# Layer 3 of a four-layer network on one core: query blocks of 10 rows in place of 8, with two reorderings of the masking

## The chip, the cores and the metric

The kernel runs on one core of a Trainium2 chip. A core has five engines that run at the same time, each with its own instruction stream: PE (TensorE, matmuls), DVE (VectorE, elementwise work), ACT (ScalarE, copies and activations), POOL (GpSimd, [...]) and SP (SyncE), which here issues nearly all DMAs. [...] The metric is the device time of one execution in microseconds. Of the kernel before there are three timed runs: 3771.21, 3783.98 and 3786.39 us; the median is 3783.98.

## The reference, cut to what matters

The input is `x` of 4 images, 256 channels, 48 x 48 pixels. Four layers each compute `x = x + layer(groupnorm(x))`. Layers 0 to 2 are convolutions (one with a per-pixel softmax over 49 taps, one with binarized and one with ternarized weights) and are not touched here. Layer 3 is a linear attention over box windows, with 8 heads of 32 channels:

```python
q = jax.nn.sigmoid(Wq x); k = jax.nn.sigmoid(Wk x); v = (Wv x) / max(norm(v), 1e-12)
Ik, Ikv = integral(k), integral(outer(k, v))            # summed-area tables
for w in (1, 2, 4):
    ws = 48 // w                                        # box of 48, 24 or 12 pixels a side
    wk, wkv = box(Ik, ws), box(Ikv, ws)                 # sums over the box around each pixel
    attn = einsum('bdhw,bdfhw->bfhw', q, wkv)
    norm = einsum('bdhw,bdhw->bhw', q, wk)
    outs.append(attn / (norm + 1e-6))
return x + (Wout concat(outs) + bout)
```

So for each query pixel and each of three window sizes, the output is the sum over all key pixels in the box of (q . k) v, divided by the sum over the box of q . k.

## The kernel before, in words

**How layer 3 computes it.** Instead of the large table of outer products, the kernel forms the scores q . k for blocks of queries against tiles of keys, multiplies them with 0/1 masks that say which keys lie in the box of which query (one mask for each window size), and multiplies the masked scores with v. The normalizers come from box sums of k alone, in a separate job.

**Tiles and blocks.** A key tile (a, c) is 8 rows by 16 columns, 128 keys on the 128 partitions; there are 6 row groups a and 3 column groups c. A query block is `RB` = 8 rows by 48 columns, 384 queries; there are 6. For each image b (4), each half of the channels ct (2, four heads each) and each query block rb, the class `Block` goes through the key tiles that any of its queries sees in the widest window. `rows_seen` and `cols_seen` give the rows and columns of the block that see something of the tile with window `wi`; `HALVES` = 24, 12, 6 are the half sizes. A tile is *near* when the smallest window sees it (`many`), otherwise *far*. `tiles_of` orders them, near and far alternating while both last, columns in the order 1, 0, 2. With 8-row blocks there are 12, 15, 18, 18, 15 and 12 tiles in the six blocks, 90 for one (b, ct), 720 in all.

**One tile.** `scores` makes, for each of two pairs of heads, a PSUM tile `s` of two banks by one matmul per head (contraction over 32 channels, four heads side by side in the array). The pool of `s` has two buffers, so each pair has one. fp32 matmuls appear in the profile as two instructions each. `masked` then makes SBUF tiles `sm0`, `sm1`, `sm2`, one per window size, for each pair:

- `copy`: where every query row and column sees the whole key tile in the widest window (`full`; columns f0 to f1), no mask is needed and ACT copies `s` to `sm0`.
- `widest`: DVE masks the remaining column strips from `s` to `sm0`. If the tile is not `full`, DVE masks all of it and ACT copies nothing.
- `middle`: for near tiles, DVE masks `s` to `sm1`.
- POOL masks the smallest window from `sm0` to `sm2` in near tiles, and the middle one from `sm0` to `sm1` in far tiles that see it.

Before the change these are issued in this order (first and second are the pairs of heads):

```python
copy(*first)
middle(*second)
copy(*second)
middle(*first)
widest(*first)
widest(*second)
```

`sums` multiplies v (32 columns per head, four heads side by side) with the masked scores and adds into three PSUM banks `acc`, one per window. It runs `LAG` = 2 tiles behind `scores`: in the main loop at the end of the file, step n issues the scores and masks of tile n, then the sums of tile n-2. [...] four by `s`, three by `acc`, one (`st`) by everything else.

**The rest of layer 3, interleaved.** Every step also calls `advance`, which moves a list of generator jobs on by one step each; a job says with `yield` how many steps it wants to pause (`FETCH` is 4). The engines then run their streams in the order of issue. The jobs are:

- `Projection` for the next image (q, k, v from x3), on PE, ACT, DVE and POOL, written to DRAM.
- `k_sums`: box sums of k (DVE scans, POOL adds), written to `kb_d`.
- `norms`, one for each 8 rows: loads the box sums above (`nhi`) and below (`nlo`), subtracts and multiplies with q on POOL for each channel half, sums over the channels of a head on PE, takes the reciprocal on DVE and writes it to `r_d`.
- `prepare` and `finish` for each block with ct = 1: load the block's other half (`o`), the residual (`res`) and the reciprocals (`rc`), multiply on DVE, then the output projection `out_ps` on PE (12 matmul calls in two pieces), add the bias and residual on DVE, and store.

`until` and `wait_for` hold the program's order of issue, not an engine: a step whose data is not yet issued advances the jobs until it is. Key tiles are loaded by `load_kv` (`ks`, `vs`) into a pool of 12 buffers each, the next half's at the points in `LOADS`; query rows by `load_q`.

Layer 3's first `s` matmul starts at 1429.5 us of the profiled execution and its last at 3751.0, so it is some 62% of the time. All helper calls carry line 142 in the profile, so groups are told apart by tile names.

Of the kernel before, what the change touches and what calls it, by code (L numbers as in the profile page):

```python
# [80 lines left out]
NKT = NRB * NKC  # L81

# [63 lines left out]
def conv_preact_kernel(  # L146
# [76 lines left out]
    o_d = [dram.tile([NRB, P, NW * NB], F32, tag=f"o{b}", name=f"o_d{b}") for b in range(B)]  # L223
    n_d = [dram.tile([NRB, HEADS, NW, NB], F32, tag=f"n{b}", name=f"n_d{b}") for b in range(B)]
    r_d = [dram.tile([NRB, HEADS, NW, NB], F32, tag=f"r{b}", name=f"r_d{b}") for b in range(B)]
# [1257 lines left out]
    with (  # L1483
        tc.tile_pool(name="wts3", bufs=1, reuse_waits="tile") as wts,
        tc.tile_pool(name="kvp", bufs=2 * NRB, reuse_waits="tile") as kvp,
# [21 lines left out]
        zeros = wts.tile([P, NB], BF16, name="zeros")  # L1507
# [63 lines left out]
        def norms(b, rb):  # L1571


            sums = []

            def load(ct):
                chans = slice(ct * P, (ct + 1) * P)
                hi = scr.tile([P, NW, RB, W], F32, tag="nhi", name="nhi")
                lo = scr.tile([P, NW, RB, W], F32, tag="nlo", name="nlo")
                qf = scr.tile([P, RB, W], F32, tag="nq", name="nq")  # L1580
                sync.dma_start(
                    out=qf.rearrange("p r w -> p (r w)"),
                    in_=q_d[b][chans, rb * NB : (rb + 1) * NB],
                )
                for wi, h in enumerate(HALVES):

                    y0 = rb * RB + h - 1
                    n = max(0, min(RB, H - y0))
                    if n > 0:
                        sync.dma_start(  # L1590
                            out=hi[:, wi, 0:n], in_=kb_d[b][wi, chans, y0 : y0 + n, :]
                        )
                    if n < RB:
                        sync.dma_start(
                            out=hi[:, wi, n:RB],
                            in_=kb_d[b][wi, chans, H - 1 : H, :].to_broadcast([P, RB - n, W]),
                        )

                    y0 = rb * RB - h - 1
                    n = min(RB, max(0, -y0))  # L1600
                    if n < RB:
                        sync.dma_start(
                            out=lo[:, wi, n:RB], in_=kb_d[b][wi, chans, y0 + n : y0 + RB, :]
                        )
                return hi, lo, qf

            last = min(rb + HALVES[0] // RB, NRB - 1)
            yield from wait_for(
                *((what, b, ct, at) for what, at in (("kb", last), ("q", rb)) for ct in range(NCT))
            )  # L1610
            loaded = [load(ct) for ct in range(NCT)]
            yield FETCH
            for hi, lo, qf in loaded:
                for wi, h in enumerate(HALVES):
                    n = min(RB, max(0, h + 1 - rb * RB))
                    if n < RB:
                        pool.tensor_sub(hi[:, wi, n:RB], hi[:, wi, n:RB], lo[:, wi, n:RB])
                yield 1
                for wi in range(NW):
                    pool.tensor_mul(hi[:, wi], hi[:, wi], qf)  # L1620
                sums.append(hi)
                yield 1
            yield 1
            yield from bank(1)
            ps = ps_m.tile([P, 512], F32, tag="st", name="norm_ps")
            for ct in range(NCT):
                for wi in range(NW):
                    pe.matmul(
                        ps[D * wi : D * (wi + 1), 0:NB],
                        head_sel[:, ct, :],  # L1630
                        sums[ct][:, wi].rearrange("p r w -> p (r w)"),
                        start=(ct == 0),
                        stop=(ct == NCT - 1),
                    )
            yield 1
            ns = scr.tile([D * NW, NB], F32, tag="ns", name="ns", bufs=1)
            act.copy(ns, ps[0 : D * NW, 0:NB])
            yield 1
            for wi in range(NW):
                sync.dma_start(out=n_d[b][rb, :, wi, :], in_=ns[D * wi : D * wi + HEADS])  # L1640
            nn = HEADS * NW * NB // P
            nr = scr.tile([P, nn], F32, tag="nr", name="nr")
            flat = [d[b][rb].rearrange("h w n -> (h w n)") for d in (n_d, r_d)]
            sync.dma_start(out=nr, in_=flat[0].rearrange("(p n) -> p n", n=nn))
            yield FETCH
            dve.tensor_scalar_add(nr, nr, ATTN_EPS)
            dve.reciprocal(nr, nr)
            yield 1
            sync.dma_start(out=flat[1].rearrange("(p n) -> p n", n=nn), in_=nr)
            made.add(("norm", b, rb))  # L1650
# [12 lines left out]
        def load_q(b, ct, rb):  # L1663
            qs = qp.tile([P, RB, W], F32, tag="qs", name="qs")
            sync.dma_start(
                out=qs.rearrange("p r w -> p (r w)"),
                in_=q_d[b][ct * P : (ct + 1) * P, rb * NB : (rb + 1) * NB],
            )
            return qs

        def rows_seen(wi, a, rb):

            h = HALVES[wi]
            return (
                max(0, a * RB - h + 1 - rb * RB),
                min(RB, a * RB + RB + h - rb * RB),
            )
# [5 lines left out]
        class Block:  # L1683


            def __init__(self, b, ct, rb, qs):
                self.b, self.ct, self.rb, self.qs = b, ct, rb, qs
                self.tiles = tiles_of(rb)
                self.todo = [
                    [(a, c) for a, c in self.tiles if seen(wi, a, rb)] for wi in range(NW)  # L1690
                ]
                self.accs = self.stage = None

# [18 lines left out]
            def masked(self, a, c, ss):  # L1712
# [8 lines left out]
                            [P, 2, RB, min(W, KC + 2 * HALVES[wi])],  # L1721
# [15 lines left out]
                def times_mask(engine, wi, rows, cols, dst, src):  # L1737
                    mr = rb * RB + rows[0] - (a * RB - HALVES[wi] + 1)
# [14 lines left out]
                full = abs(a - rb) * RB + RB <= HALVES[0]  # L1753
# [7 lines left out]
                def copy(s, tiles):  # L1761
                    if full:
                        act.copy(
                            view(tiles, 0, (r0, r1), (f0, f1)), s[:, :, :, f0 - c0 : f1 - c0]
                        )

                def widest(s, tiles):
# [3 lines left out]
                    for p0, p1 in ((c0, f0), (f1, c1)):  # L1771
                        if p0 < p1:
                            of_banks(s, tiles, 0, (r0, r1), (p0, p1))

# [4 lines left out]
                middle(*second)  # L1779
                copy(*second)  # L1780
                middle(*first)
                widest(*first)
# [13 lines left out]
            def begin(self):  # L1796
                self.accs = [
                    ps_acc.tile([P, NB], F32, tag=f"acc{i}", name=f"acc{i}") for i in range(NW)
                ]
                self.stage = op.tile([P, NW, NB], F32, tag="stage", name="stage")  # L1800

                for acc in self.accs[1:]:
                    pe.matmul(acc, zeros[:, 0:P], zeros, start=True, stop=False)
# [23 lines left out]
        def tiles_of(rb):  # L1827
# [4 lines left out]
                for a in sorted(range(NRB), key=lambda a: abs(a - rb))  # L1832
# [8 lines left out]
        def prepare(i):  # L1841

            b, ct, rb = order[i]
            yield from wait_for(("norm", b, rb))
            yield from take("o")
            o = op.tile([P, NW, NB], F32, tag="o", name="o", bufs=1)
            sync.dma_start(out=o.rearrange("p w n -> p (w n)"), in_=o_d[b][rb])
            yield from take("res")
            res = scr.tile([P, NCT, RB, W], F32, tag="res", name="res")
            sync.dma_start(  # L1850
                out=res,
                in_=x3_d[b][:, rb * RB : (rb + 1) * RB, :].rearrange("(ct p) r w -> p ct r w", p=P),
            )
            rcs = []
            for t in range(NCT):
                yield from take("rc")
                rc = op.tile([P, NW, NB], F32, tag="rc", name="rc")
                for g in range(HG):
                    sync.dma_start(
                        out=rc[g * D : (g + 1) * D].rearrange("p w n -> p (w n)"),  # L1860
                        in_=r_d[b][rb, t * HG + g]
                        .rearrange("w n -> (w n)")
                        .partition_broadcast(D),
# [4 lines left out]
        def finish(i, stage):  # L1868


            b, ct, rb = order[i]
            yield 1
            if ct == 0:
                sync.dma_start(out=o_d[b][rb], in_=stage.rearrange("p w n -> p (w n)"))
# [11 lines left out]
            for mo in range(NCT):  # L1886
                yield from bank(2)
                ps = ps_m.tile([P, 512], F32, tag="st", name="out_ps")[:, 0:NB]
# [18 lines left out]
                out=out[b, :, rb * RB : (rb + 1) * RB, :].rearrange("(ct p) r w -> p ct r w", p=P),  # L1907
# [4 lines left out]
        order = [(b, ct, rb) for b in range(B) for ct in range(NCT) for rb in range(NRB)]  # L1912
# [11 lines left out]
        seen_first = HALVES[0] // RB + 1  # L1924
# [6 lines left out]
        LOADS = {2: (0,), 3: (1, 2), 4: (3, 4), 5: (5,)}  # L1931
# [20 lines left out]
        def midway(i):  # L1952

            b, ct, rb = order[i]
            if (b, ct) == (0, 0) and 0 < rb <= NRB - seen_first:
                a = seen_first - 1 + rb
                until(("k", 0, 0, a), ("v", 0, a))
                load_kv(0, 0, a)
            if ct == NCT - 1:
                start(prepare(i))  # L1960
            if i + 1 < len(order):
                nb, nct, nrb = order[i + 1]
                until(("q", nb, nct, nrb))
# [88 lines left out]
```

## Time and profile before

| What | Value |
|---|---|
| Median of three runs | 3783.98 us |
| Profiled execution | 3777.16 us |
| Span from first to last instruction | 3775.4 us |
| Mean granted TensorE clock | 0.952 |
| PE / DVE / ACT / POOL busy | 3264.8 / 2487.2 / 1036.2 / 1518.1 us |
| Layer 3, `s` matmuls | 5760, 832.5 us |
| Layer 3, `acc` matmuls from `sm` | 13440, 880.5 us |
| Layer 3, DVE masks | 2592, 1135.8 us |
| Layer 3, ACT copies `sm<-s` | 1152, 594.9 us |
| Layer 3, POOL masks | 1152, 853.3 us |

In the lines of the profile, `out<-in` are the program's tile names, then come partitions x elements and type of output and input, the count, the busy time in us, the mean of one in ns, and the idle time of the engine just before such instructions with what ended most of it. Busy time counts overlapping instructions of one engine once, so it can be less than count times mean. A line of the timeline gives start, length and engine of a run of equal instructions, and in brackets the idle time before it with its releaser. A line of the waits reads: who waited for whom, us in total, times, longest. A line of the table by stretches gives, after its length, busy us and instructions of PE, PE's weight loads, DVE, ACT and POOL, then the granted clock, the DMA share and GB/s.

### The profile page before, as it was taken

The numbers are of one execution on the slowest core, as the hardware profiler recorded it, in microseconds if no ns is written. First come the engines' busy times: TensorE is split into PE (matmuls) and PEld (weight loads), VectorE is DVE, ScalarE is ACT, GpSimd is POOL, SyncE is SP. The second block draws the span as 40 slices with busy tenths as digits, with TensorE's granted clock in tenths as the row PEclk, the third lists the DMA queues.
The fourth block names the chain that finished last, engine by engine and source line by source line (L and its number), as shares of the span: only waits on it lengthen the run. The fifth ranks groups of instructions, "written<-read, shape, count | busy, mean of one in ns | idle before, by whom it ended". The sixth has DMA issues, their size and how long they took to land. (4 is left out here: it accounts for less than half of the span.)

```text
span 3775.4 us, 68847 instructions
## 1 busy us (share of the span) xinstructions
PE 3264.8 (86%) x26498; PEld 1879.4 (50%) x26498; DVE 2487.2 (66%) x5119; ACT 1036.2 (27%) x2025; POOL 1518.1 (40%) x2184
## 2 busy tenths in 40 slices
PE   3688898998996788988889889899899899989998
PEld 2467686786784564433334334344443344444443
DVE  7876587587583366777666567756577766556665
ACT  0012111111113322433222333332344332233331
POOL 0000120020020034778765486755365766344332
PEclk9798999999997899999999899999999999999999
DMA  7745323324324313345434243533223444101122
GB/s 250 238 135 170 100 104 116 109 95 125 109 75 124 102 70 108 125 136 159 125 103 131 90 136 122 164 97 108 78 95 123 139 116 116 47 31 53 41 60 60
DMA packets 373019, 423.04 MB, mean 112 GB/s; under 512 B 129076, under 2 KB 328532, under 8 KB 371540
## 3 DMA queue, kind: packets, MB, share of 16 engines
q1 hardware_dynamic: 371491, 416.32, 35.6%
q8 instruction: 211, 3.46, 0.4%
q0 software_dynamic: 144, 1.52, 0.2%
q14 instruction: 117, 0.95, 0.1%
q10 hardware_dynamic: 1056, 0.79, 0.1%
HBM read 288.79 MB, written 131.25 MB: 111 GB/s over the span
## 5 line engine op out<-in xcount | busy, mean ns | idle before, releaser
L142 DVE TENSOR_TENSOR sm<-s,masks 128x112 f32<-128x112 f32 (+10 forms) x2592 | 1135.8, 493 | 765.5 <-PE s L142 321.1
L142 POOL TENSOR_TENSOR sm<-sm,masks 128x432 f32<-128x432 f32 (+14 forms) x1152 | 853.3, 755 | 936.5 <-ACT sm L142 672.0
L142 PE MATMUL s<-qs,ks 32*128 32x320 f32 (+3 forms) x5760 | 832.5, 500 | 200.1 <-DVE sm L142 151.2
L142 ACT COPY sm<-s 128x528 f32<-128x528 f32 (+2 forms) x1152 | 594.9, 535 | 1470.7 <-PE s L142 1169.9
L142 PE MATMUL acc<-sm,vs 128*32 128x384 f32 (+18 forms) x13440 | 880.5, 385 | 16.1 <-POOL sm L142 15.8
L142 PEld LDWEIGHTS s<-qs,ks 32*128 32x128 f32 x5760 | 374.1, 185 | 604.7 <-DVE sm L142 232.8
L142 PE MATMUL cv<-vx,wt 128*128 128x288 f32 x2080 | 559.3, 425 | 90.7 <-DVE vx L142 49.1
L142 PEld LDWEIGHTS acc<-sm,vs 128*32 128x32 f32 x13440 | 355.2, 110 | 551.3 <-issue 348.6
L142 PEld LDWEIGHTS cv<-vx,wt 128*128 128x128 f32 x2080 | 402.4, 198 | 212.4 <-issue 53.6
L142 POOL MEMSET v<- 128x16 f32 (+1 forms) x120 | 18.6, 215 | 725.7 <-DVE vx L142 635.7
L142 PE MATMUL cv<-v,wl 128*128 128x384 f32 x1152 | 224.5, 354 | 24.4 <-DVE x L142 9.2
L142 PEld LDWEIGHTS cv<-v,wl 128*128 128x128 f32 x1152 | 214.8, 195 | 34.6 <-issue 16.1
L142 POOL TENSOR_TENSOR pt<-pt 128x144 f32<-128x144 f32 x336 | 187.4, 558 | 22.8 <-DVE pt L142 0.5
L142 POOL TENSOR_TENSOR v<-l2v,v 128x384 fp32r<-128x384 f32 x96 | 109.2, 1168 | 130.2 <-ACT v L142 121.4
L142 POOL TENSOR_TENSOR nhi<-nhi,nq 128x384 f32<-128x384 f32 x144 | 148.3, 1058 | 0.0
L142 PE MATMUL cv<-pad,wl 128*128 128x384 bf16 x864 | 143.1, 327 | 0.0
L142 PE MATMUL out_ps<-o,wout_sb 128*128 128x384 f32 x288 | 122.8, 509 | 9.4 <-DVE o L142 5.4
L142 PE MATMUL out_ps<-stage,wout_sb 128*128 128x384 f32 x288 | 117.3, 489 | 0.4 <-DVE stage L142 0.4
L142 PE MATMUL proj_ps<-wv_sb,xn 128*128 128x256 f32 x288 | 89.5, 438 | 32.3 <-ACT vt L142 19.1
L142 DVE TENSOR_TENSOR vx<-v 128x868 f32<-128x868 f32 x112 | 115.4, 1056 | 0.5
L142 PE MATMUL ap<-seen,xT 120*128 120x120 f32 (+3 forms) x832 | 113.5, 293 | 0.0
L142 PEld LDWEIGHTS <-wl 128*128 128x128 bf16 x864 | 83.8, 97 | 59.1 <-issue 0.4
(162 smaller groups left out, 2859.0 us busy)
## 6 DMA issues: line engine op xcount, KB each, us to landing
wt<-wt SPq DMA_DIRECT2D x48, 768.0 KB
kb_d<-pt SPq DMA_DIRECT2D x48, 576.0 KB
rc<-r_d SPq DMA_DIRECT2D x192, 144.0 KB
nhi<-kb_d SPq DMA_DIRECT2D x120, 192.0 KB
nlo<-kb_d SPq DMA_DIRECT2D x88, 192.0 KB
o_d<-stage SPq DMA_DIRECT2D x24, 576.0 KB
o<-o_d SPq DMA_DIRECT2D x24, 576.0 KB
wl<-wl_d SPq DMA_DIRECT2D x16, 768.0 KB
```

The lines of the kernel that those rows point to most:

```text
L142: return lambda *args, **kwargs: self.tc.keep_in_program_order(op(*args, **kwargs))
```

## The change

Three edits, all in layer 3.

1. Query blocks have `QR` = 10 rows (480 queries) in place of 8: five blocks, of rows 0-10, 10-20, 20-30, 30-40 and 40-48. Key tiles stay at 8 rows. Buffers, the DRAM layouts of `o_d` and `r_d`, loads, masks and the output projection follow the block size. The `norms` job stays at 8 rows; its result goes to the new layout of `r_d` in eight DMAs, one for each head, in place of one.
2. The block no longer has to be wholly inside the region that needs no mask. Of the rows of a tile, those from g0 to g1 see all of it; if they are over a third of the rows, ACT copies them and DVE masks the rows above and below.
3. The order of masking: both copies first, then the middle masks of the first and of the second pair.

With it go smaller buffers: key tiles 9 in place of 12, `nlo` and `nr` 1 in place of 2. `nlo` of the second channel half is therefore loaded after the first half's subtraction, and `norms` pauses for `FETCH` steps between the halves. Blocks with 10 rows have 15, 18, 18, 18 and 12 tiles, 81 for one (b, ct), 648 in all.

```diff
+QR = 10
+QROWS = [(y, min(H, y + QR)) for y in range(0, H, QR)]
+NQB = len(QROWS)
+QN = QR * W
...
-    o_d = [dram.tile([NRB, P, NW * NB], F32, tag=f"o{b}", name=f"o_d{b}") for b in range(B)]
+    o_d = [dram.tile([NQB, P, NW, QN], F32, tag=f"o{b}", name=f"o_d{b}") for b in range(B)]
...
-    r_d = [dram.tile([NRB, HEADS, NW, NB], F32, tag=f"r{b}", name=f"r_d{b}") for b in range(B)]
+    r_d = [dram.tile([HEADS, NW, HW], F32, tag=f"r{b}", name=f"r_d{b}") for b in range(B)]
...
-        tc.tile_pool(name="kvp", bufs=2 * NRB, reuse_waits="tile") as kvp,
+        tc.tile_pool(name="kvp", bufs=NRB + 3, reuse_waits="tile") as kvp,
...
+            def load_less(ct):
+
+                chans = slice(ct * P, (ct + 1) * P)
+                lo = scr.tile([P, NW, RB, W], F32, tag="nlo", name="nlo", bufs=1)
+                for wi, h in enumerate(HALVES):
...
             loaded = [load(ct) for ct in range(NCT)]
+            lo = load_less(0)
             yield FETCH
-            for hi, lo, qf in loaded:
+            for ct, (hi, qf) in enumerate(loaded):
+                if ct > 0:
+                    yield FETCH
                 for wi, h in enumerate(HALVES):
                     n = min(RB, max(0, h + 1 - rb * RB))
                     if n < RB:
                         pool.tensor_sub(hi[:, wi, n:RB], hi[:, wi, n:RB], lo[:, wi, n:RB])
+                if ct + 1 < NCT:
+                    lo = load_less(ct + 1)
                 yield 1
...
-            sync.dma_start(out=flat[1].rearrange("(p n) -> p n", n=nn), in_=nr)
+            for h in range(HEADS):
+                sync.dma_start(
+                    out=r_d[b][h, :, rb * NB : (rb + 1) * NB].rearrange("w (s n) -> w s n", n=nn),
+                    in_=nr[h * NW * 4 : (h + 1) * NW * 4],
+                )
...
             h = HALVES[wi]
-            return (
-                max(0, a * RB - h + 1 - rb * RB),
-                min(RB, a * RB + RB + h - rb * RB),
-            )
+            y0, y1 = QROWS[rb]
+            return max(0, a * RB - h + 1 - y0), min(y1, a * RB + RB + h) - y0
...
-                full = abs(a - rb) * RB + RB <= HALVES[0]
+                g0 = max(r0, a * RB + RB - HALVES[0] - self.y0)
+                g1 = min(r1, a * RB + HALVES[0] + 1 - self.y0)
+                full = 3 * (g1 - g0) > r1 - r0
...
                         act.copy(
-                            view(tiles, 0, (r0, r1), (f0, f1)), s[:, :, :, f0 - c0 : f1 - c0]
+                            view(tiles, 0, (g0, g1), (f0, f1)),
+                            s[:, :, g0 - r0 : g1 - r0, f0 - c0 : f1 - c0],
                         )
...
                     for p0, p1 in ((c0, f0), (f1, c1)):
                         if p0 < p1:
-                            of_banks(s, tiles, 0, (r0, r1), (p0, p1))
-
+                            of_banks(s, tiles, 0, (g0, g1), (p0, p1))
+                    for p0, p1 in ((r0, g0), (g1, r1)):
+                        if p0 < p1:
+                            of_banks(s, tiles, 0, (p0, p1), (c0, c1))
...
                 first, second = zip(ss, pairs)
                 copy(*first)
-                middle(*second)
                 copy(*second)
                 middle(*first)
+                middle(*second)
                 widest(*first)
                 widest(*second)
...
-                for a in sorted(range(NRB), key=lambda a: abs(a - rb))
+                for a in sorted(range(NRB), key=lambda a: abs(2 * a * RB + RB - sum(QROWS[rb])))
...
-        seen_first = HALVES[0] // RB + 1
+        last_key = [min(NRB - 1, (y1 + HALVES[0] - 2) // RB) for _, y1 in QROWS]
+        seen_first = last_key[0] + 1
...
-        LOADS = {2: (0,), 3: (1, 2), 4: (3, 4), 5: (5,)}
+        LOADS = {1: (0,), 2: (1, 2), 3: (3, 4), 4: (5,)}
```

## The prediction

> **What bounds the kernel now.** I read the totals by engine first, then the table by stretches, then the order of time inside one stretch, then the waits. The groups of the profile page (busy us, mean ns | idle before) say who does what in layer 3:
>
> ```profile
> L142 DVE TENSOR_TENSOR sm<-s,masks 128x112 f32<-128x112 f32 (+10 forms) x2592 | 1135.8, 493 | 765.5 <-PE s L142 321.1
> L142 POOL TENSOR_TENSOR sm<-sm,masks 128x432 f32<-128x432 f32 (+14 forms) x1152 | 853.3, 755 | 936.5 <-ACT sm L142 672.0
> L142 PE MATMUL s<-qs,ks 32*128 32x320 f32 (+3 forms) x5760 | 832.5, 500 | 200.1 <-DVE sm L142 151.2
> L142 ACT COPY sm<-s 128x528 f32<-128x528 f32 (+2 forms) x1152 | 594.9, 535 | 1470.7 <-PE s L142 1169.9
> ```
>
> PE looks busy (220.61 of 245.20 us in the stretch below), but its `s` matmuls wait for DVE. The order of time shows why: one near tile (start 3329.37) and one far tile (3332.83), middle columns:
>
> ```profile
> 3329.37 1.29 PE L142 MATMUL s<-qs,ks 32*128 32x384 f32 x8
> ...
> 3330.39 0.61 ACT L142 COPY sm<-s 128x528 f32<-128x528 f32 x1 [1.15 <-PE s L142]
> ...
> 3330.59 1.40 PE L142 MATMUL acc<-sm,vs 128*32 128x216 f32 x24
> 3330.78 2.28 DVE L142 TENSOR_TENSOR sm<-s,masks 128x624 f32<-128x624 f32 x6 [1.09 <-PE s L142]
> ...
> 3331.68 0.61 ACT L142 COPY sm<-s 128x528 f32<-128x528 f32 x1 [0.68 <-DVE sm L142]
> ...
> 3332.83 1.29 PE L142 MATMUL s<-qs,ks 32*128 32x384 f32 x8 [0.83 <-DVE sm L142]
> 3333.84 1.12 ACT L142 COPY sm<-s 128x528 f32<-128x528 f32 x2 [1.54 <-PE s L142]
> ...
> 3334.49 0.80 DVE L142 TENSOR_TENSOR sm<-s,masks 128x128 f32<-128x128 f32 x3 [1.42 <-ACT sm L142]
> ```
>
> Each pair of heads has one score buffer, so the next `s` starts when the first pair's buffer has been read: 3.46 us after the last start for this near tile, 2.28 for the far one. In between PE does the sums of two tiles ago and idles 0.83. Layer 3 is a chain PE to ACT/DVE to PE. ACT's second copy waited 0.68 for DVE, which only reads the same scores. The stretch of batch 3, channels 0 has no projections and no norms:
>
> ```profile
> 3233.70:3478.90 245.20, 220.61 (x2438) 100.79 (x2438) 147.36 (x334) 81.25 (x162) 102.60 (x144) 0.99 0.13 40
> ```
>
> 245.2 us for 90 tiles; two starts there carry an output-projection piece (6.95 and 6.69 us against 3.07 and 3.1 for their like), so 237.7 without them. The stall rows that the rest can move:
>
> ```profile
> ACT sm L142 <- DVE sm L142: 235.9, 349, 3.8
> PEld acc L142 <- POOL sm L142: 57.7, 118, 3.8
> PEld norm_ps L142 <- POOL nhi L142: 19.9, 27, 1.9
> ```
>
> [...] the copy starts just after DVE's mask ends. [...] PE is at 90% and still waits for buffers. [...] The trace: a DVE mask takes 0.265 us at 112 elements and 0.952 at 768, so 0.148 + 1.047 ns per element alone, about 0.07 + 1.047 ns started behind another.
>
> **The change part by part.** Lengths used: first ACT copy after its `s` start 0.905 us at 320 columns, 1.02 at 384 (timeline), hence 1.05 at 400 and 1.19 at 480 (estimates on that line). Copies 0.480, 0.509, 0.615 at 384, 400, 528 elements, hence 0.565, 0.60, 0.73 at 480, 500, 660.
>
> *Count.* Per batch and channel half there are 90 tiles before, 81 after; in triples of column tiles: 16 near, 8 far, 6 edge (all masked by DVE) before; after 15 near, 6 far (3 of them copied in 4 to 6 of 10 rows), 6 edge, of 9, 1, 3, 10, 2 and 8 rows. Score columns are the same (237 query rows times three). But blocks of 10 are not aligned to key tiles of 8: rows inside near tiles go from 128 to 13x10+2x8 = 146, and a near row is the dear one. PE issues 576 fewer `s` and 1728 fewer `acc` matmuls; I cost that at nothing, since PE waits within the chain (if PE were the limit: rival d). DVE has 96 fewer masks but 44,000 more elements per partition (46 us of work), ACT 144 fewer copies.
>
> *Near tile, 10 rows, new order.* Middle mask of the first pair now waits for its copy [...]: start at 1.19+0.73+0.03 = 1.95, two masks of 780 at 0.892 each, two strips (160, 140) 0.53, release to PE 0.14: 4.40 us. Left and right columns: 1.05+0.60+0.03+2x0.66+0.465+0.15 = 3.615, and 3.56. A triple costs 11.58; 13 make 150.5, less 2.4 for six rows that window 1 does not see. Two 8-row triples: 9.68 before (average of the quiet stretch), 9.79 after, since copy-then-mask starts DVE 0.11 to 0.25 later than second-pair-first after a far tile. Near: 167.7 against 154.9.
>
> *Far and edge.* Full far triple 7.05 (2.27+1.92+1.89 = 6.1 at 8 rows, longer copies and columns), two of them; 6.1 once; three partly copied, where DVE takes the other rows (576 elements, 0.67 us, in place of a copy): 7.35 each. Sum 42.3 against 48.8. Edge, by the same line (8 rows 5.6 in the trace): 6.55+6.05+5.6, and for 3, 2 and 1 rows, where PE's sums of two tiles ago set the pace, 4.1+3.75+4.5: 30.6 against 32.6. After an edge or partly copied tile the second pair's scores come 0.85 late, which delays mask two: 2.3. New bank openings: 0.8 (in the old averages already). Total 243.7 against 237.7, eight times: **+48 us**.
>
> *Inserted PE work.* Column counts of output, norm and projection matmuls don't change. Of their time near tiles hide the slack between chain and PE. Chain grows by 0.94, 0.57, 0.65, PE's own path by about 0.4, so 0.3 more per insert on some 100 near inserts: **-30** (ends: 0 if ACT's and DVE's share of an insert eats it, -42). But when an insert frees both buffers at once, the old order started DVE 0.4 earlier in a following near tile; copy-first can't: 56 inserts on far tiles, **+22** (ends 0, +25).
>
> *GpSimd.* 240 fewer masks, 36,000 fewer elements; middle-window work goes to DVE (in the sum above). Two norm halves, each about 2x1.1+3x1.06 us of POOL, ran in four consecutive steps; FETCH between them lets POOL catch up. Of 24 norm starts, the tiles cost 71 us over their like, with 33 of PE work in it; I take **-20** (ends 0, and -60 if every POOL stall named above goes).
>
> *Queues and buffers.* Norms issue 7 more DMAs each, 168 on SP at 0.3 to 0.5 us (timeline: `qs` 0.37 to 0.42): about 70 us of SP, over 2300; hidden. `lo` with one buffer makes SP wait for POOL's subtraction, behind it `qs`, `ks`, `vs`, `rc`; those are issued 7 or more tiles (20 us) ahead, so a wait of a few us is covered. Without cover each of 24 would cost what POOL is behind, up to 3 us: +70. With 9 key buffers the earliest reuse is key tile 0 after query block 3, loaded 12 tiles before use: covered. Startup loads five key tiles for four: the wait shown there is on the third, unchanged. Norms now take about 20 steps for 16, 120 of a batch's 162: still ahead of the blocks that need them.
>
> Sum: 48-30+22-20 = **+20 us** on the profiled span of 3775.4, so 3795, its execution 3797. The shown median is 6.8 above that execution (3777.16 against 3783.98): 3804.
>
> **Rivals.**
> (a) *GpSimd relief wins (faster).* Place: sums waiting for masks and norms. For it: 57.7+19.9 us of PE waits on POOL, and masks that POOL ends 9 us after their scores beside a norm (3.3 otherwise; timeline at 2976). Against: nearly half of the norm tiles' extra is PE's own matmuls. It decides once the relief exceeds 40 us; at -60 the sum is -20: 3764.
> (b) *Covers fail (slower).* No extra hiding, no relief, late second pairs as estimated: 48+22 = +70, or up to +140 if SP blocks behind the norm. Against: loads run far ahead. 3854.
> (c) *The swap doesn't serialize.* DVE masks while ACT copies the same pair; near tiles then fall to PE's path, 0.1 to 0.7 us less on 360 tiles, -170: 3634. Against: the 0.68 wait.
> (d) *PE was the bound after all*: [...] 3768. Against: PE's idle before `s`, 200 us.
>
> **How the numbers follow.** Forecast (net -20 to +60) 0.50: of it 0.30 slower, 0.18 same, 0.02 faster. (b) 0.27, slower. (a) 0.13, faster but 0.02 same. (d) 0.05, half same. (c) 0.03; rest 0.02. Half a per cent, 19 us, is about what a measurement here tells from no change. Slower 0.58, same 0.22, faster 0.20. The range goes from 3735 (a with all its relief) to 3890; the forecast's own is 3764 to 3844.
>
> **What would show it.** Right: 648 starts of `s`; near middle tiles at 4.4 us, side ones at 3.6, DVE's first mask 0.03 after the copy ends; the quiet stretch (no projection, no norm) near 244 us for 81 tiles; the row ACT sm <- DVE sm almost gone, DVE sm <- ACT sm grown; POOL's masks at about 730 us. Wrong: DVE starting with the copy, a quiet stretch under 237, PE's waits on POOL unchanged, or new waits of `s` or `acc` on loads.

## The result and the profile after

The changed kernel takes 3924.39 us (median of four runs, 3921.63 to 3929.78) against 3785.18 for the kernel before beside it: 1.0377 times as long, 95% interval 1.0348 to 1.0406. The forecast of 3804 and the upper end of 3890 were both too low; the sign was right. The profiled execution takes 3927.07, its span 3925.3 us, so the span grew by 150 where the sum had 20.

The groups of layer 3 on the page of the changed kernel (all helper calls carry line 146 now):

```profile
L146 DVE TENSOR_TENSOR sm<-s,masks 128x160 f32<-128x160 f32 (+18 forms) x2496 | 1165.8, 524 | 879.6 <-ACT sm L146 668.3
L146 POOL TENSOR_TENSOR sm<-sm,masks 128x540 f32<-128x540 f32 (+28 forms) x912 | 721.9, 808 | 1193.0 <-ACT sm L146 1041.1
L146 PE MATMUL s<-qs,ks 32*128 32x400 f32 (+11 forms) x5184 | 844.2, 561 | 344.9 <-DVE sm L146 304.5
L146 ACT COPY sm<-s 128x660 f32<-128x660 f32 (+14 forms) x1008 | 548.4, 583 | 1568.8 <-PE s L146 1106.9
```

Hardly any work was added: DVE's masks are 30 us longer, POOL's 131 shorter, ACT's copies 46 shorter. What grew is waiting: DVE's idle time before a mask ended by ACT went from 266.9 (in the waits of before) to 668.3 us, and PE's idle before `s` from 200.1 to 344.9. The waits of the changed kernel in layer 3 (who waited for whom, us in total, times, longest):

```profile
DVE sm L146 <- ACT sm L146: 668.3, 469, 6.2
PE s L146 <- DVE sm L146: 304.5, 289, 14.7
...
DVE o L146 <- DMA rc<-r_d: 42.0, 4, 15.7
PEld acc L146 <- POOL sm L146: 38.1, 111, 2.6
...
ACT sg L146 <- DMA q_d<-sg: 25.4, 5, 11.2
...
POOL nhi L146 <- DMA nlo<-kb_d: 20.8, 8, 6.6
```

The row in which ACT's copies waited for DVE (235.9 us before) is gone, and PE waits less for POOL (57.7 before). Three rows are new in size: DVE waits for the reciprocals `rc` (5.1 before), ACT, in the projections, for stores of q to land (5.5 before), and POOL for the box sums `nlo` (no such row before). The table by stretches for batch 3, channels 0, where 245.20 us stood before:

```profile
3356.08:3613.23 257.15, 221.95 (x2172) 92.59 (x2171) 153.69 (x327) 76.87 (x143) 110.55 (x138) 0.97 0.22 62
```

PE has nearly the same work (221.95 against 220.61) in 12 us more; the granted clock is 0.97 where it was 0.99. Two norm pieces now fall into this half. One near tile in it, middle columns, after a far one, in order of time:

```profile
3547.47 1.33 PE L146 MATMUL s<-qs,ks 32*128 32x480 f32 x8
3548.64 1.35 ACT L146 COPY sm<-s 128x660 f32<-128x660 f32 x2 [1.50 <-PE s L146]
...
3549.40 2.73 DVE L146 TENSOR_TENSOR sm<-s,masks 128x780 f32<-128x780 f32 x6 [1.73 <-ACT sm L146]
...
3551.84 0.67 PE L146 MATMUL s<-qs,ks 32*128 32x480 f32 x2 [1.42 <-DVE sm L146]
```

One copy of this size takes 0.73 (a line of the best run below has it alone), so the first ends at 3549.37. DVE starts 0.03 later, 1.93 after the scores (the working had 1.95), and the next scores come 4.37 after the last (the working had 4.40).

The worst of the new waits, SP's queue and then the same place on DVE and on PE (start, length; in brackets the idle time and its releaser):

```profile
2012.39 5.74 SPq L146 DMA_DIRECT2D r_d<-nr  x8
...
2021.75 3.69 SPq L146 DMA_DIRECT2D nhi<-kb_d  x4
2025.48 1.48 SPq L146 DMA_DIRECT2D nlo<-kb_d  x3
...
2027.96 7.50 SPq L146 DMA_DIRECT2D rc<-r_d  x8
```
```profile
2037.91 0.66 DVE L146 TENSOR_TENSOR o<-o,rc 128x480 f32<-128x480 f32 x1 [15.73 <-DMA rc<-r_d]
```
```profile
2038.94 1.75 PE L146 MATMUL s<-qs,ks 32*128 32x320 f32 x8 [14.72 <-DVE sm L146]
```

The multiplication of `o` stands in DVE's stream ahead of masks. Its reciprocals are loaded only when SP has issued the eight stores of the norm and the next norm's box sums. From 2025 to 2039 us the 16 DMA engines are busy throughout, too (share 1.01; table by stretches at the end), so the loads that come together here may also hold each other up, and the order on SP's queue need not be the whole cause of this wait. For 15.73 us DVE does nothing, and PE has no free score buffer.

### The profile page after: what moved, and what is told of

Same layout as the page of the kernel before. It is cut to its first block, busy times and chain, and to the rows that moved or that the text cites. A ratio compares the mean times of both kernels' runs of the same rounds, so it can differ in the third digit from the quotient of the medians.

```text
span 3925.3 us, 63350 instructions
## 1 busy us (share of the span) xinstructions
PE 3298.3 (84%) x24082; PEld 1811.8 (46%) x24082; DVE 2498.8 (64%) x4991; ACT 992.7 (25%) x1857; POOL 1375.8 (35%) x1944
## 5 line engine op out<-in xcount | busy, mean ns | idle before, releaser
L146 DVE TENSOR_TENSOR sm<-s,masks 128x160 f32<-128x160 f32 (+18 forms) x2496 | 1165.8, 524 | 879.6 <-ACT sm L146 668.3
L146 POOL TENSOR_TENSOR sm<-sm,masks 128x540 f32<-128x540 f32 (+28 forms) x912 | 721.9, 808 | 1193.0 <-ACT sm L146 1041.1
L146 PE MATMUL s<-qs,ks 32*128 32x400 f32 (+11 forms) x5184 | 844.2, 561 | 344.9 <-DVE sm L146 304.5
L146 ACT COPY sm<-s 128x660 f32<-128x660 f32 (+14 forms) x1008 | 548.4, 583 | 1568.8 <-PE s L146 1106.9
L146 PE MATMUL acc<-sm,vs 128*32 128x400 f32 (+25 forms) x11712 | 905.9, 435 | 2.5 <-POOL sm L146 2.5
L146 PEld LDWEIGHTS s<-qs,ks 32*128 32x128 f32 x5184 | 358.8, 195 | 711.0 <-issue 404.5
L146 PEld LDWEIGHTS acc<-sm,vs 128*32 128x32 f32 x11712 | 323.1, 114 | 652.2 <-issue 533.1
L146 PE MATMUL out_ps<-o,wout_sb 128*128 128x480 f32 (+1 forms) x240 | 119.1, 579 | 8.2 <-DMA rc<-r_d 6.1
L146 PE MATMUL out_ps<-stage,wout_sb 128*128 128x480 f32 (+1 forms) x240 | 114.2, 558 | 0.2 <-DVE stage L146 0.2
L146 DVE SCALAR_TENSOR_TENSOR x<-cv,alpha,x 128x384 f32<-128x384 f32 x144 | 83.9, 610 | 41.8 <-PE cv L146 41.5
```

The source lines that it names most:

```text
L146: return lambda *args, **kwargs: self.tc.keep_in_program_order(op(*args, **kwargs))
```

## The experiments

Each set of runs has its own runs of the kernel before beside it, and the sets differ by some us, so differences are taken between ratios; one per cent is about 38 us. "Measured" gives for each run the median in us, the ratio to the kernel before beside it, and the 95% interval of that ratio. My first theory after the result was that the order of masking costs time in the chain, and more with longer blocks; the first rival was that the blocks or the side work cost it. To split a half's time I also use a *cleaned* quiet half: the lengths of the 90 or 81 tiles of batch 3, channels 0, where a tile with an inserted output or norm piece counts with the median of its like. It is 237.0 us in the kernel before and 246.1 in the changed one, where the prediction had 237.7 and 243.7. These sums depend on which tiles are called alike: with those of the same kind and column, and norm or output matmuls as the mark of an inserted piece, they are 237.7 and 246.7, and other runs move by up to 1.7, some 14 us over the eight halves. They are estimates from one half each.

**The order of masking, undone and alone.** `a_old_order` is the changed kernel with the old order, `b_new_order` the kernel before with the new one (the edit shown is the first; the second is its reverse):

```diff
                 copy(*first)
-                copy(*second)
-                middle(*first)
                 middle(*second)
+                copy(*second)
+                middle(*first)
```

> The changed kernel (3924) with the masks issued in the order of before: copy first pair, middle second, copy second, middle first. Theory 1, the order is a main loss: at 10 rows DVE starts 0.15 to 0.25 us earlier in near tiles after a far tile, about -30 us over layer 3, and ACT's other jobs (table loads, sigmoids) no longer hold DVE at the head of a tile, another -30: 3865. Theory 2, block size and pacing carry the loss: after tiles with late second pairs the old order loses what it gains elsewhere, within 15 us of 3924.

> The kernel before (3785) with only the masking order changed: both copies, then the middle masks of first and second pair. Theory 1: near middle tiles 3.71 us for 3.46, side ones 3.06 and 3.01 for 3.04 and 2.92 after far tiles, and inserted projections and output pieces dearer: +50 to +80, 3835 to 3865. Theory 2: the quiet stretch alone pays, +10 to +30, 3795 to 3815.

Measured: 3836.91, ratio 1.0141 (1.0099 to 1.0184), and 3840.89, 1.0146 (1.0113 to 1.0179). The order costs 57 us at 8 rows and about 89 (1.0377 less 1.0141) at 10. The cleaned quiet half agrees about as well as it can: 243.3 to 245.0 for the kernel before with the new order (6.3 to 7.4 more, eight times 50 to 59), 232.5 to 234.2 for the changed one with the old order (11.9 to 14.2 less, eight times 95 to 114). It also says that 10-row blocks shorten the chain if the order stays, 234.2 against 237.0 (232.5 against 237.7 by the other choice).

**The copies of part of the rows.** `a_all_rows` lets ACT copy only where all rows see the whole tile:

```diff
-                full = 3 * (g1 - g0) > r1 - r0
+                full = g1 - g0 == r1 - r0
```

> The changed kernel with ACT copying only where all rows of a far tile see the whole key tile, so DVE masks all of the nine partly copied tiles of each half. Theory: a DVE mask of the whole takes less time than copy, strips and rows one after another (2.53 against 2.71 us for the middle column in the quiet stretch, 2.1 to 2.2 against 2.38 for the side ones), -10 to -20 us: 3905 to 3915. Rival, ACT's share relieves DVE: +10 to +20.

Measured: 3905.53, 1.0331 (1.0289 to 1.0373): some 17 us, as expected, though the intervals overlap.

**The block size.** `a_rb8` is the changed kernel with blocks of 8 rows and the loading points of the kernel before:

```diff
-QR = 10
+QR = 8
...
-        LOADS = {1: (0,), 2: (1, 2), 3: (3, 4), 4: (5,)}
+        LOADS = {2: (0,), 3: (1, 2), 4: (3, 4), 5: (5,)}
```

> The changed kernel with blocks of 8 rows again (QR = 8 and the load points of before), all its other edits kept: order of masking, norms split, eight reciprocal DMAs, smaller buffers. Theory 1: apart from the order, what costs is the 10-row block itself (fewer tiles to spread the same jobs over): as the kernel before with the new order, 3841 within 10. Theory 2: the edits to norms, DMAs and buffers cost on their own: 3870 to 3900.

Measured: 3858.58, 1.0197 (1.0176 to 1.0218), between the two. Against the new order alone (1.0146) there are 19 us more (the intervals just touch), though with whole tiles of 8 rows next to nothing but the edits to norms, DMAs and buffers is left. And from here to the changed kernel there are 68 more.

**The norms split, alone.** `b_norm_split` puts the split norm (`load_less`, one `nlo` buffer, the pause between the halves) into the kernel before, with its one store:

```diff
             loaded = [load(ct) for ct in range(NCT)]
+            lo = load_less(0)
             yield FETCH
-            for hi, lo, qf in loaded:
+            for ct, (hi, qf) in enumerate(loaded):
+                if ct > 0:
+                    yield FETCH
...
```

> The kernel before with the norms job alone changed: the second half's box sums loaded after the first half's subtraction, and a pause of FETCH steps between the halves. Theory: GpSimd catches up between the halves, tiles with norm matmuls cost 35 us over their like in all in place of 71: -20 to -35, 3750 to 3765. Rival: the stalls come from elsewhere or the later norms hold the output projections: within 10 us of 3785.

Measured: 3779.94, 0.9992 (0.9977 to 1.0007). The relief is not there in the total. The tiles with norm work did get shorter, from about 70 us over their like to between 40 and 46, which was the predicted mechanism; the rest of the stream took the time back.

**Late reciprocals.** `a_late_finish` lets `prepare` pause eight more steps before it hands the loaded block to the multiplication:

```diff
+            yield 2 * FETCH
             prepared[i] = o, res, rcs
```

> The changed kernel with one line: the prepare job pauses eight steps between issuing the loads of rc and letting finish issue the DVE multiplications that read them. Theory 1: part of the loss is that the norms of the first image come late, so DVE stands 15.7, 14.8 and 5.8 us in front of a load with the masks behind it: -30 to -40, 3885 to 3895. Theory 2: those stalls are covered by something else that is late, or the delay moves the stall to the next block: within 10 us of 3924.

Measured: 3906.85, 1.0329 (1.0308 to 1.035): 18 us less (the intervals just touch), about half of what I expected. The half of batch 0 with the 15.73 us above fell from 350.2 to 320.9 us, but the next one rose from 330.2 to 350.7, where projections and output pieces now met.

**A third order.** Each pair's middle mask ahead of its copy, since the chain should be shorter so; `b_mid_first` in the kernel before, `a_mid_first` in the changed one (with the full copies and the later finish), `b_mid_first_split` with the split norms (the edit is shown against the old order):

```diff
-                copy(*first)
-                middle(*second)
-                copy(*second)
                 middle(*first)
+                copy(*first)
+                middle(*second)
+                copy(*second)
```

> The kernel before with the order middle first, copy first, middle second, copy second, then the widest masks. Theory: the chain of a near tile starts with whoever reads the first pair first; here DVE starts as soon as the first pair's scores are there, 0.4 us ahead of the old order and 0.5 to 0.6 ahead of the new. Near tiles: 3.06 us for the middle column, 2.55 for the right, PE-bound 2.95 for the left; about -0.28 us on 384 tiles, -80 to -110: 3675 to 3705. Rival, PE's sums or GpSimd's later start take the place of the chain: -20 to 0, 3765 to 3785.

> The changed kernel with that order, with ACT copying only where all rows see the tile, and with the late multiplications. Sum of the parts: order -150 to -175, copies -19, loads -35: 3695 to 3720 from 3924. If the 10-row block is worth something once the order is right, it is below the 8-row kernel with the same order; if its denser jobs eat that, 10 to 40 us above it.

> The kernel before with each pair's middle mask ahead of its copy, and the norms in two halves. With the order alone the quiet half fell by 7.2 us and the whole rose by 18. Theory 1 (what took the gain back was GpSimd's burst of work at the norms, which the split spreads): 3740 to 3775. Theory 2 (the gain is taken back by DVE, which with this order has less time before the next pair's scores whatever GpSimd does): 3790 to 3810.

Measured: 3803.08, 1.005 (1.0034 to 1.0065); 3851.11, 1.0173 (1.0141 to 1.0204); 3809.98, 1.0071 (1.0042 to 1.0101). The first two took longer than any figure forecast for them; the third lies at the upper end of its theory 2. A near tile of the first, in order of time:

```profile
3359.70 1.21 PE L142 MATMUL s<-qs,ks 32*128 32x384 f32 x8
3360.73 1.96 DVE L142 TENSOR_TENSOR sm<-s,masks 128x624 f32<-128x624 f32 x4 [0.79 <-POOL sm L142]
...
3362.84 1.63 PE L142 MATMUL s<-qs,ks 32*128 32x384 f32 x8 [0.60 <-DVE sm L142]
```

The chain is shorter as thought: 3.14 us from scores to scores, 3.46 in the kernel before, and the cleaned quiet half falls from 237.0 to 229.8. Yet the whole is 19 us longer: tiles with projection pieces exceed their like by some 41 us more than before, those with norms by 7 to 8 more. With the norms split it is not better, so POOL's burst is not what takes the gain back. What does, was not settled. In the changed kernel this order is no better: against `a_best10` below, which differs from `a_mid_first` in the order alone, it costs 56 us (1.0173 against 1.0025).

**The eight stores.** `a_old_rb8` leaves of the change only the edits to norms, DMAs and buffers (8 rows, old order). `a_one_store` is the changed kernel with one store, `a_old_rb8_one` the first of these with one store:

```diff
-            for h in range(HEADS):
-                sync.dma_start(
-                    out=r_d[b][h, :, rb * NB : (rb + 1) * NB].rearrange("w (s n) -> w s n", n=nn),
-                    in_=nr[h * NW * 4 : (h + 1) * NW * 4],
-                )
+            sync.dma_start(
+                out=r_d[b]
+                .rearrange("h w x -> (h w) x")[:, rb * NB : (rb + 1) * NB]
+                .rearrange("g (s n) -> g s n", n=nn),
+                in_=nr,
+            )
```

> The changed kernel with 8-row blocks, the loading points of 8-row blocks and the old order of masking: of the change only the edits to norms, their DMAs and the buffers are left. Theory 1 (these edits cost what the 8-row version of the change cost over the kernel before with the new order alone, some 17 us, because the eight stores and the split norm put DVE and PE behind late loads): 3795 to 3810. Theory 2 (they are free as the prediction had it, and cost only next to the new order): 3780 to 3790.

> The changed kernel with the reciprocals of a norm stored by one DMA in place of eight; all else as changed. Theory 1 (the eight stores hold SP's queue, 5.74 us in one place, and the loads of the reciprocals behind them come late, so that DVE and then PE stand, 15.7 us in the worst place): 3900 to 3912 against 3924. Theory 2 (what makes the reciprocals late is the norm's longer path of some 20 steps, not SP): within 8 us of 3924.

> The changed kernel with 8-row blocks and the old order of masking (measured 3802.0, the kernel before 3781.5), and the reciprocals of a norm stored by one DMA in place of eight. Theory 1 (the eight stores are what the norm and buffer edits cost): 3778 to 3788. Theory 2 (the cost is the split norm, whose POOL work and channel sums fall on other tiles, and the single buffer of box sums): 3796 to 3806.

Measured: 3802.0, 1.0055 (1.0041 to 1.0069); 3897.84, 1.0301 (1.0263 to 1.0338); 3774.54, 0.9984 (0.9968 to 1.0). The eight stores cost 27 us in the one kernel and 29 in the other, and the rest of the edits to norms and buffers nothing. How: in the first of the three, SP's queue at one norm, and what POOL does there:

```profile
2486.77 5.74 SPq L146 DMA_DIRECT2D r_d<-nr  x8
...
2497.20 5.72 SPq L146 DMA_DIRECT2D nlo<-kb_d  x4
```
```profile
2500.62 1.47 POOL L146 TENSOR_TENSOR nhi<-nhi,nlo 128x144 f32<-128x144 f32 x2 [6.03 <-DMA nlo<-kb_d]
```

The loads of the next norm stand behind the stores of the last one. They land after POOL has come to the subtraction, and POOL's masks stand behind that. POOL's waits for `nlo`, with eight stores and with one:

```profile
POOL nhi L146 <- DMA nlo<-kb_d: 33.1, 13, 6.0
```
```profile
POOL nhi L146 <- DMA nlo<-kb_d: 0.2, 1, 0.2
```

In the changed kernel one store takes away more than the waits for `nlo` (20.8 to 3.4 us): those for `rc` fall from 42.0 to 28.6, and those of ACT for stores of q from 25.4 to 7.8.

**What is left.** `a_best10` is the changed kernel with the old order, full copies and the later finish; `a_old_ar_one` has the old order, full copies and one store; `a_best10_one` has all four.

> The changed kernel with the old order of masking, copies only where all rows see the whole tile, and the finish of a block two pauses later. If the three costs add (87 for the order, 19 for the copies, 17 for the late loads) it takes 3795 to 3810. Theory 1 (they add, and 10-row blocks alone cost no more than some 20 us over the kernel before): 3795 to 3815. Theory 2 (they overlap, since each frees work that then waits for the next late engine): 3820 to 3836, as with the old order alone.

> The changed kernel with the old order of masking, copies only where all rows see the whole tile, one store of the reciprocals, and the finish of a block where the change has it. If the three add (87, 19 and 26 below 3924): 3785 to 3800. Theory 1 (the stores were what made the reciprocals late, so a later finish isn't needed): within 8 us of the version that has both, or below it. Theory 2 (the later finish is needed too): 10 or more above it.

> As the run without it, with one store of the reciprocals and also the later finish. With eight stores this took 3791.5 against 3781.5 for the kernel before. Theory 1 (the stores' cost is apart from that of the early finish): 3765 to 3780, faster than both kernels. Theory 2 (the later finish had already hidden the late reciprocals, so one store gains nothing more): 3785 to 3795.

Measured: 3791.49, 1.0025 (1.0011 to 1.0038); 3791.48, 1.0039 (1.0026 to 1.0052); 3758.58, 0.9941 (0.992 to 0.9962). The stores and the early finish are two causes, since each mended alone leaves 32 to 37 us that go when both are: with both gone the kernel is 0.6% faster than the kernel before, the best of the study. Without the later finish, DVE still waits in the second:

```profile
DVE o L146 <- DMA rc<-r_d: 25.9, 3, 11.5
```

In the best one that wait is 4.2 us. Its tile for the near one shown above (same place, 4.37 there), and its stretch of batch 3, channels 0:

```profile
3388.82 1.44 PE L146 MATMUL s<-qs,ks 32*128 32x480 f32 x8
3389.99 0.73 ACT L146 COPY sm<-s 128x660 f32<-128x660 f32 x1 [1.39 <-PE s L146]
...
3390.37 2.73 DVE L146 TENSOR_TENSOR sm<-s,masks 128x780 f32<-128x780 f32 x6 [1.25 <-POOL sm L146]
...
3391.43 0.73 ACT L146 COPY sm<-s 128x660 f32<-128x660 f32 x1 [0.71 <-DVE sm L146]
...
3392.81 0.67 PE L146 MATMUL s<-qs,ks 32*128 32x480 f32 x2 [0.93 <-DVE sm L146]
```
```profile
3207.67:3452.45 244.78, 220.63 (x2170) 91.90 (x2170) 155.38 (x302) 73.13 (x125) 104.90 (x132) 0.98 0.18 53
```

DVE's 2.73 us are the same in both tiles. With the old order they begin 1.55 after the scores, on the second pair while ACT copies the first; with the new one 1.93. That is the 0.38 us between 3.99 and 4.37.

**Each part put back alone.** `a_old_part` is the best one with the copies of part of the rows, `a_new_fixed` the best one with the new order. `b_late_finish` is the kernel before with the later finish.

> The version that took 3758.6 (old order, one store, later finish), but with the copies of part of the rows as in the change. Theory 1 (they cost some 19 whatever the order): 3770 to 3785. Theory 2 (they cost only with the new order, since with the old one the quiet half took 243.4 with them and 244.8 without): 3750 to 3765.

> The version that took 3758.6, but with the change's order of masking (both copies first). Theory 1 (the order costs 87 at 10-row blocks, as where it was undone alone): 3835 to 3855. Theory 2 (part of the 87 was that the order met late loads and stalled stores, and they are gone): 3800 to 3825.

> The kernel before, with the finish of a block two pauses later. With 10-row blocks, the old order and one store, this delay is worth 33 us (3791.5 to 3758.6). Theory 1 (the delay mends what the change did: the norms end later and the loads of the reciprocals with them): within 8 us of 3781. Theory 2 (it is a gain of its own that the kernel before could have had): 3745 to 3770.

Measured: 3765.63, 0.9961 (0.9951 to 0.9972); 3856.35, 1.0198 (1.0183 to 1.0213); 3806.62, 1.007 (1.0044 to 1.0097). The partial copies cost 8 us, if anything (the intervals overlap). The order costs 97. And the later finish, worth 37 us at 10-row blocks with one store, costs 26 in the kernel before: it is no gain that the kernel before could have had, and neither theory foresaw a cost there. Why it costs was not looked into.

## Why the prediction was wrong

The miss is 130 us on the span (20 forecast, 150 measured).

**Right: the chain's mechanism.** DVE waits for the copy of the same pair, 0.68 us of waiting turned round. Near middle tiles of 10 rows take a median of 4.34 us in the quiet half and 4.37 in the tile shown (4.40 worked out), side ones 3.57 and 3.52 (3.615 and 3.56), and POOL's masks 721.9 us (about 730). That the two engines take turns on one pair's scores is measured here, not explained: in the kernel before, ACT's second copy starts 0.09 us after the end of DVE's mask of that pair (3331.68, the mask being 0.81 from 3330.78); in the tile above, DVE starts 0.03 us after the copy's end, with that copy as its releaser; and the row DVE sm <- ACT sm has grown to 668.3 us. The rival that the swap doesn't serialize is out.

**A size: +48.** The cleaned quiet halves give 246.1 less 237.0, times eight: 73. By kinds the near tiles nearly fit (171 to 172 against 167.7 and the 3.1 for late second pairs and bank openings). Partly copied and far tiles took 43 to 44 for 42.3, edge tiles 31.1 for 30.6. The term was 25 too low. Some 11 of these are in the sum itself: the parts listed for the kernel before, 154.9, 48.8 and 32.6, make 236.3, and the total subtracts 237.7. What I had not seen is that it was two terms of opposite sign, about +95 for the order and -22 for the blocks (+114 and -41 by the other choice of like tiles). I priced only their sum, so nothing in the text says that the order alone loses more than the whole forecast.

**The step that failed first: "about 70 us of SP, over 2300; hidden."** It asked how full SP's queue is, not what stands in it and when. The length was off as well: I took 0.3 to 0.5 us from loads of `qs`, and these stores take 0.67 (table below), 129 us in all. They come as one run of 5.74 us just ahead of the next norm's loads and of `rc`, and cost 29 us. "A wait of a few us is covered" failed for `nlo`, which POOL needs four steps after its issue; the price that I gave for lost cover, up to 3 us for each norm, 70 in all, was too high but in the right place.

**The next: "Norms now take about 20 steps for 16 ... still ahead of the blocks that need them."** The later finish is worth 18 us in the changed kernel, 37 with the stores mended, and costs 26 in the kernel before; with it DVE's wait for `rc` falls from 42.0 to 5.7 us in the changed kernel. So there the reciprocals do come late for the blocks that need them. I checked that they keep pace over a batch, not when the first block of a half asks for its reciprocals. I watched for loads that block `s` and `acc`; the wait sits on DVE's multiplication, in front of masks.

**The gains that did not come: -30 and -20.** The norm split alone changes the total by -0.23% to +0.07%, although the tiles with norm work get 24 to 29 us shorter. In the changed kernel too the mechanism is there, PE's norm matmuls wait 2.0 us for POOL where they waited 19.9, and the gain isn't. The 30 us of output and projection work hidden in longer near tiles can be read from `a_new_fixed`, which has the new order, full copies and no late loads: 75 us above the kernel before. Its cleaned quiet half is 243.9, so some 55 of them are chain (60 by the other choice), and 15 to 20 remain for everything else where I had 22 less 50. Both terms had an end of 0 in the text, and those were the ones to take. That the total shows no gain is measured for the norm split; for the output and projection work it is an estimate from this remainder.

**A term that the prediction did not have: the clock.** In both traces the clock records of TensorE hold two values alone, full and half speed. In layer 3 it was at half speed for 364 us in the changed kernel's trace and 120 in that of the kernel before; over the layers ahead of it the mean is 0.92 in both. The growth of layer 3, 158 us from first to last `s`, splits accordingly. If each tile counts with the median length of its like at full clock, the tiles account for 65 us. Those without inserted matmuls that touch a stretch at half clock exceed that by 108 us where they exceeded it by 25, so 84 more; such tiles at full clock exceed it by hardly more than before (19 against 17), and those with inserted matmuls grew by 9. Some of the waits for DMA are among the 84 (the 15.73 us above, for one), and so is what the lower clock adds after them (shown at the end). No run holds the clock fixed, so the two can't be told apart here, and the terms below contain both. In the norm split alone the same group grew by 29 us in its one trace, about what the norm tiles had gained.

Together: 25 of chain, 29 of stores, 18 of late finish and 50 of gains make 122 of the 130. The terms do not add exactly (the later finish is 18 or 37 us with and without the eight stores). Rival (b), covers fail, named this: 70 for no relief and up to 140 if SP blocks. With the late loads mended and full copies the measurement is 75, as changed 139. That the totals come so close is in part luck: its chain was 25 too low, and the stores cost 29 where it had up to 70. It had 0.27 where it deserved the most. Rival (a) falls with the split alone, which gives nothing, and (d) with the 89 us that the order of the masks is worth on the same matmuls.

## What to carry to other kernels

Price each reordering and each change of size as a term of its own, even if the sum is what is asked; two large terms of opposite sign are a kernel to be had, here, with the late loads mended, 0.6% faster than the kernel before. For every DMA that is added, list what is issued next on the same queue and which engine's stream stands behind the data (here DVE's, for 15.73 us), at the moment of issue and not as a share of the span. Count relief on an engine off the chain as nothing until a run shows otherwise.

## What the runs showed of the hardware

The time that SP's queue spent on storing one norm's `nr` went far more by the number of DMAs and their form than by bytes: 5.74 us for eight, 0.78 and 0.32 for one with the same data. The answers for the tensor `r_d` (durations in ns: least, median, most) of the kernel before, the changed kernel and the changed kernel with one store:

```profile
L142 SPq DMA_DIRECT2D r_d<-nr x24: 319/320/1228, 1645.2 to 3206.8; - x24
```
```profile
L146 SPq DMA_DIRECT2D r_d<-nr x192: 669/672/816, 1680.9 to 3507.3; - x192
```
```profile
L146 SPq DMA_DIRECT2D r_d<-nr x24: 765/780/873, 1698.5 to 3479.1; - x24
```

A store of 12 partitions to three rows of DRAM takes 0.672 us, one of all 96 partitions to 24 rows, eight times the data, 0.780; the flat store of before took 0.320.

The long wait of PE shown above costs more than its length, since the clock stays low after it. The table by stretches of the changed kernel around the wait of 14.72 us (after the length: busy us and instructions of PE, PE's weight loads, DVE, ACT, POOL; then the granted clock, the DMA share, GB/s), and eight `s` matmuls of 320 columns ahead of it:

```profile
2020.00:2025.00 5.00, 4.23 (x54) 1.53 (x50) 1.79 (x4) 1.78 (x4) 2.20 (x3) 1.00 0.96 219
2025.00:2039.00 14.00, 0.06 (x2) 0.06 (x2) 1.09 (x3) 0.00 (x0) 0.03 (x1) 0.56 1.01 268
2039.00:2045.00 6.00, 6.00 (x56) 2.63 (x56) 4.18 (x8) 1.48 (x4) 6.00 (x7) 0.60 0.55 129
2045.00:2050.00 5.00, 3.70 (x44) 1.94 (x40) 4.77 (x10) 1.37 (x3) 5.00 (x6) 1.00 0.50 153
```
```profile
2019.01 1.32 PE L146 MATMUL s<-qs,ks 32*128 32x320 f32 x8 [0.91 <-ACT sm L146]
```

The clock falls during the wait and is back at full speed only some 5 us after it; the first eight `s` matmuls after it, of the same size, take 1.75 us for 1.32. Of the 59 stretches at half clock in layer 3 of this trace 27 last 3.41 us, the shortest length there, and the others two, three or five times that. In the 3.41 us ahead of each of them PE was busy for 71% at most (46% in the median); that this is what lowers the clock is not shown.

And a shorter chain need not be a shorter kernel: with the middle mask ahead of the copy the quiet tiles were 3% faster and the whole 0.5% slower.
